# Layer 2's scan: tokens loaded one step ahead, first map of the preparation at tile 2

## The chip, the cores and the metric

The kernel runs on 1 core of one Trainium2 chip. The metric is device microseconds of one execution. In the profile PE is TensorE's matmul track, PEld its weight loads, DVE is VectorE, ACT ScalarE, POOL GpSimd, SP SyncE (here it only issues DMAs). L1548 is line 1548 of the kernel before.

## The reference

Four layers run one after the other on `x` of shape (8, 64, 64, 64), float32: a spectral convolution, a four-way selective scan with a feed-forward part, a second selective scan (the layer that is changed here) and a last layer with scans along both axes. The part of layer 2 that matters:

```python
def spa_ssm(x, in_w, conv_w, conv_b, xproj_w, dt_w, dt_b, Alog, D, out_w):
    xz = xs @ in_w                                   # xs: (8, 4096, 64), 2 x 128 out
    xi, z = (xz[..., :di], xz[..., di:])             # di = 128
    xi = silu(causal_dwconv1d(xi, conv_w, conv_b))   # 4 taps
    dbc = xi @ xproj_w                               # 4 + 16 + 16
    dt = softplus(dbc[..., :dtr] @ dt_w + dt_b)
    B, C = dbc[..., dtr:dtr + 16], dbc[..., dtr + 16:]
    A = -exp(Alog)                                   # (128, 16)
    # h = exp(dt * A) * h + (dt * xi) * B ;  y = sum over the 16 states of h * C
    y = selective_scan(exp(dt[..., None] * A), (dt * xi)[..., None] * B[:, :, None, :], C) + D * xi
    y = y * silu(z)
    return (y @ out_w).reshape(b, h, w, c)
```

## The kernel before

Layer 2's scan (`l2_scan`) cuts the 8 images of 4096 tokens into 32 steps of T = 1024 tokens (image `b`, chunk `c`). The 128 inner channels lie on the partitions. Each step has 16 tiles, one for each state `n`; a tile is 128 x 1024. The loop over all 512 tiles is in `stream`, and it writes the order of the work out by hand (`tc.manual_schedule()`): each engine runs its instructions in the order in which the program issues them.

For tile `i` the work is:

- SP loads a row of B and a row of C, spread over all partitions (`load`, line 1583, 1 MB, into one of 8 buffers `bc`). The load for tile `i + 6` is issued at tile `i`.
- POOL multiplies `du` with B into one of 4 buffers `hb` (line 465), three tiles ahead.
- ACT makes the decay `dA = exp(dt * A)` in one of two PSUM tiles (line 472), two tiles ahead.
- DVE runs the scan (line 481).
- The product with C (line 495) is DVE's in 11 tiles and POOL's in the five of `shared = (1, 4, 7, 10, 13)`.
- From chunk 0 to 2 of an image, ACT copies the last column into the next chunk's `carry` (line 1592).
- PE adds the product to the step's sum `acc` in PSUM, by a matmul with the identity (`gather`, line 287), two tiles later. `acc` is a single buffer: at tile 2 of the next step DVE drains it into `z` (line 1601), and PE starts the new sum with the skip product of `u`. In this one tile the gather is issued behind the scan, in the others ahead of it.

Beside this, a step prepares the next one. `prepare` is a generator, and `stream` starts it at the tile `n == start` and takes one piece of it per tile. A piece that ends in `yield CALM` holds the next piece back until a calm tile, that is, until neither this tile nor the next one is in `shared` (2, 5, 8, 11, 14, 15). The pieces and their tiles are:

| Tile | Piece |
|---|---|
| 1 | Load the tokens `x0` (two DMAs on SP; in chunk 0 also two small memsets on POOL), `yield False` |
| 2 | Nothing (`yield`) |
| 3 | First map: 4 taps and input projection in one, 4 matmuls into the PSUM tile `mm` (line 1548, eight rows of the profile), `yield CALM` |
| 5 | `u` = Silu of it on ACT (line 1551, with a table load), matmul to `dbc` |
| 6 | Copy to `dbl` (1556), B and C to HBM by two DMAs on ACT's queue (1559), matmul to `dt` |
| 8 | `dt` = Softplus (line 396, with a table load) |
| 9 | `du` = `dt * u` on POOL (1569), matmul to `z` (1573) |
| 11 | `z` = Silu (1579, with a table load) |

Once `prepare` is over, the gate of the step before the current one (output matmuls of `z` and of the residual from `x0`, copy by ACT at line 1513, store) runs at tiles 11 to 14. It uses the same single PSUM tile `mm`. The exponential of the decays needs ACT's table again after each of `u`, `dt` and `z`.

Of the kernel before, what the change touches and what calls it, by code (L numbers as in the profile page):

```python
# [10 lines left out]
F32 = mybir.dt.float32  # L11
# [11 lines left out]
T = 1024  # L23
# [226 lines left out]
class Net:  # L250
# [1228 lines left out]
    def l2_scan(self, hx, hy):  # L1479
        nc, tc, d = self.nc, self.tc, self.d  # L1480
        with ExitStack() as ctx:
            pool = lambda n, b, **k: ctx.enter_context(tc.tile_pool(name="l2" + n, bufs=b, **k))
            cp, p1, p2, tp = pool("c", 1), pool("p1", 1), pool("p2", 2), pool("t", 2)
            pp = pool("pp", 1, space=PSUM)
            pools = (pool("bc", 8), pool("hb", 4), pool("hc", 4), pool("h", 3), pool("pe", 2, space=PSUM), pool("pa", 1, space=PSUM))
            hp = pool("h3", 3, space=DRAM)
            w_in, cb, xp, dtw, dtb, A, D, w_out = (
                self.load(cp, "l2_" + n) for n in ("in", "cb", "xp", "dtw", "dtb", "A", "D", "out")
            )
            self.minus_exp(A)  # L1490
            skip = self.diag(cp, "skip", D, 1)

            taps = cp.tile([128, 2, 128], F32, name="taps")
            for m in range(2):
                for r in range(2):
                    j = 3 - 2 * m - r
                    nc.sync.dma_start(taps[r * C : r * C + C, m, :], d["l2_taps"][j : j + 1, :].to_broadcast([C, 128]))
                nc.vector.tensor_tensor(taps[:, m, :], taps[:, m, :], w_in[:, :128], ALU.mult)

            def gate(b, c, y, x0):  # L1500
                q, half = b // 2, slice((b % 2) * C, (b % 2) * C + C)
                yield
                ps = pp.tile([128, T], F32, name="mm")
                self.mm(ps[:C], w_out, y, start=True, stop=False)
                for r in range(2):
                    at, f = slice(r * C, r * C + C), 3 + r + r * 512
                    nc.tensor.matmul(
                        ps[:C, r * 512 : r * 512 + 512], self.ident2[at, :C], x0[at, f : f + 512], start=False, stop=True
                    )
                yield True  # L1510
                yield True
                o = tp.tile([C, T], F32, name="tmp")
                nc.scalar.copy(o, ps[:C])
                nc.scalar.dma_start(hy[q, half, c * T : c * T + T], o)

            carries = {}

            class Step:
                bc_shape, start, early, late = [128, 2, T], 1, 0, False
                shared = (1, 4, 7, 10, 13)  # L1520
                rev = False
                shaped = staticmethod(lambda t: t)
                spread = staticmethod(lambda t, m: t[:, m, :])
                lanes = [(slice(None), A)]

                def __init__(self, b, c):
                    self.b, self.c = b, c

                def ready(self):
                    pass  # L1530

                def prepare(self):
                    b, c = self.b, self.c

                    x0 = self.x0 = p2.tile([128, T + 4], F32, name="x0", bufs=3)
                    for r in range(2):
                        lo = c * T - 3 - r
                        if c == 0:
                            nc.gpsimd.memset(x0[r * C : r * C + C, : 3 + r], 0.0)
                        skip_ = max(0, -lo)  # L1540
                        nc.sync.dma_start(x0[r * C : r * C + C, skip_ : T + 3 + r], hx[b, :, lo + skip_ : c * T + T])
                    yield False
                    yield
                    px = pp.tile([128, T], F32, name="mm")
                    for o in (0, 512):
                        for m in range(2):
                            f = o + 3 - 2 * m
                            nc.tensor.matmul(px[:, o : o + 512], taps[:, m, :], x0[:, f : f + 512], start=m == 0, stop=m == 1)  # L1548
                    yield CALM
                    u = self.u = p2.tile([128, T], F32, name="u")  # L1550
                    nc.scalar.activation(u, px, AF.Silu, bias=cb)
                    pd = pp.tile([128, T], F32, name="mm")[:68]
                    net.mm(pd, xp, u)
                    yield True
                    dbl = p1.tile([68, T], F32, name="dbl")
                    nc.scalar.copy(dbl, pd)
                    self.bc = hp.tile([NS, 2, T], F32, name="bc")
                    for m in range(2):
                        nc.scalar.dma_start(self.bc[:, m, :], dbl[4 + m * NS : 4 + m * NS + NS])
                    pt = pp.tile([128, T], F32, name="mm")  # L1560
                    for r in range(2):
                        at, o = slice(r * C, r * C + 4), slice(r * 512, r * 512 + 512)
                        nc.tensor.matmul(pt[:, o], dtw[at], dbl[at, o], start=True, stop=True)
                    yield CALM
                    dt = self.dt = p2.tile([128, T], F32, name="dt")
                    net.softplus_act(dt, pt, dtb)
                    yield
                    du = self.du = p2.tile([128, T], F32, name="du")
                    nc.gpsimd.tensor_tensor(du, dt, u, ALU.mult)
                    pz = pp.tile([128, T], F32, name="mm")  # L1570
                    for r in range(2):
                        at, f = slice(r * C, r * C + C), 3 + r + r * 512
                        nc.tensor.matmul(
                            pz[:, r * 512 : r * 512 + 512], w_in[at, 128:], x0[at, f : f + 512], start=True, stop=True
                        )
                    yield True
                    yield CALM
                    z = self.z = p2.tile([128, T], F32, name="z", bufs=3)
                    nc.scalar.activation(z, pz, AF.Silu)

                def load(self, n, t):
                    row = self.bc[n : n + 1].rearrange("o m t -> o (m t)")
                    nc.sync.dma_start(t.rearrange("p m t -> p (m t)"), row.to_broadcast([128, 2 * T]))

                def first(self, n):
                    if n == 0:
                        self.carry = p2.tile([128, NS], F32, name="carry") if self.c < 3 else None
                    return carries[self.b][:, n : n + 1] if self.c else 0.0

                def keep(self, n, h):  # L1590
                    if self.carry is not None:
                        nc.scalar.copy(self.carry[:, n : n + 1], h[:, T - 1 : T])
                    if n == NS - 1:
                        carries[self.b] = self.carry

                def skip(self, acc):
                    net.mm(acc, skip[:, 0, :], self.u, start=True, stop=False)
                    return True

                def drain(self, acc):  # L1600
                    nc.vector.tensor_tensor(self.z, acc, self.z, ALU.mult)

                def done(self):
                    net.urgent.append(Task(gate(self.b, self.c, self.z, self.x0)))

            net = self
            with tc.manual_schedule():
                steps = [Step(b, c) for b in range(NB) for c in range(4)]
                self.stream(pools, (6, 3, 6), steps, deque())

    def leaky(self, out, ps):
# [432 lines left out]
```

## Time and profile before

| | |
|---|---|
| Median of 3 runs | 25221.08 us (25216.33 to 25233.35) |
| Profiled execution, its own time | 25231.76 us |
| Its span, first to last instruction | 25229.9 us |
| Busy shares of the span: PE, DVE, ACT, POOL | 85%, 89%, 58%, 87% |
| First and last `DMA_DIRECT2D` of layer 2's token load (line 1541) | 9133.4 and 10797.8 us |
| First and last drain of layer 2's scan (line 1601) | 9220.9 and 10905.2 us |

The profile is of one execution. A busy share is an average over four layers with different limits, so what bears on a change is read from the stretch in which its lines run. A wait "A L1 <- B L2" means that engine A sat idle ahead of its instruction of line L1 until B finished one of line L2. Names stand without their numbers: `x0` appears as `x`.

### The profile page before, as it was taken

The page shows a single profiled execution, that of the slowest core. Times are in us where ns is not written, and L with a number is a line of the kernel's source. Part 1 is how long each engine was busy: PE and PEld are TensorE (multiplying, and loading weights), DVE is VectorE, ACT ScalarE, POOL GpSimd, SP SyncE. Part 2 cuts the span into 40 slices and gives each one's busy share as a digit, 9 for nine tenths or more (in the row PEclk, how much of TensorE's full clock was granted, in tenths as well). Part 3 has the DMA queues.
Part 4 walks back from the last instruction along what each step waited for, and adds up shares of the span by engine and source line. Part 5 has one row for each costly group of instructions (what it writes and reads, how often), then busy time and mean ns, then how long its engine had stood idle before and what let it go on. Part 6 is the DMA issues. An engine that isn't in the chain of part 4 may idle for free. (4 is left out here: it accounts for less than half of the span.)

```text
span 25229.9 us, 193412 instructions
## 1 busy us (share of the span) xinstructions
PE 21360.9 (85%) x53146; PEld 8333.8 (33%) x53146; DVE 22529.7 (89%) x13020; ACT 14745.3 (58%) x18562; POOL 22031.7 (87%) x10775
## 2 busy tenths in 40 slices
PE   8777888888888888888888888888878888888888
PEld 5522333333333323322333333333323333333333
DVE  4379989989989769978999999999989999999999
ACT  4344555555555455524666666666656666666666
POOL 0089999999999759976999999999989999999999
PEclk9888999999999999989999999999989999999999
DMA  2279898889898758842555555555545555555554
GB/s 60 77 279 321 310 317 311 311 313 316 307 315 311 251 194 323 324 134 79 167 170 169 171 166 171 169 170 167 167 155 169 168 170 168 170 168 171 167 171 157
DMA packets 1772400, 5282.72 MB, mean 209 GB/s; under 512 B 536352, under 2 KB 542564, under 8 KB 1703472
## 3 DMA queue, kind: packets, MB, share of 16 engines
q1 hardware_dynamic: 1744176, 5207.00, 61.0%
q10 hardware_dynamic: 27136, 63.34, 0.8%
q8 instruction: 423, 6.93, 0.1%
q14 instruction: 665, 5.45, 0.1%
HBM read 5112.85 MB, written 156.11 MB: 209 GB/s over the span
## 5 line engine op out<-in xcount | busy, mean ns | idle before, releaser
L465 POOL TENSOR_TENSOR hb<-du,bc 128x1024 f32<-128x1024 f32 x4608 | 10749.6, 2357 | 495.7 <-DVE h L481 334.4
L287 PE MATMUL acc<-hc,ident 128*128 128x512 f32 x18816 | 8878.8, 613 | 85.8 <-DVE img L1228 55.9
L472 ACT ACTIVATE dA<-dt,w_A 128x512 f32<-128x512 f32 x8192 | 5662.8, 691 | 4111.9 <-DVE hc L495 3125.9
L481 DVE TENSOR_TENSOR_SCAN dA<-dA,hb 128x1024 f32<-128x1024 f32 x3384 | 7726.0, 2283 | 282.5 <-ACT dA L472 118.4
L287 PE MATMUL acc<-h,ident 128*128 128x512 f32 x7808 | 4553.3, 713 | 2368.4 <-POOL h L495 2368.3
L287 PEld LDWEIGHTS acc<-hc,ident 128*128 128x128 f32 x18816 | 3689.4, 200 | 5292.2 <-issue 4656.8
L465 POOL TENSOR_TENSOR hb<-du,b 128x1024 f32<-128x1024 f32 x2048 | 4869.0, 2402 | 495.0 <-DVE h L481 253.7
L495 DVE TENSOR_TENSOR hc<-dA,bc 128x1024 f32<-128x1024 f32 x3296 | 4034.2, 1224 | 260.8 <-issue 8.9
L472 ACT ACTIVATE dA<-dt,w_l_A 128x1024 f32<-128x1024 f32 x2560 | 2856.5, 1117 | 1187.5 <-DVE hc L495 761.8
L481 DVE TENSOR_TENSOR_SCAN dA<-dA,carry,hb 128x1024 f32<-128x1024 f32 x1320 | 3093.9, 2344 | 172.9 <-ACT carry L1211 111.0
L287 PEld LDWEIGHTS acc<-h,ident 128*128 128x128 f32 x7808 | 1546.1, 215 | 5028.1 <-POOL h L495 3162.1
L481 DVE TENSOR_TENSOR_SCAN h<-dA,hb 128x1024 f32<-128x1024 f32 x1352 | 3081.5, 2279 | 46.0 <-ACT dA L472 40.3
L495 POOL TENSOR_TENSOR h<-h,bc 128x1024 f32<-128x1024 f32 x1312 | 3090.1, 2355 | 14.2 <-DVE h L481 14.2
L495 DVE TENSOR_TENSOR hc<-dA,c 128x1024 f32<-128x1024 f32 x1408 | 1722.5, 1223 | 115.6 <-DMA c<-bc 4.6
L495 POOL TENSOR_TENSOR h<-h,c 128x1024 f32<-128x1024 f32 x640 | 1511.9, 2362 | 8.6 <-ACT carry L1211 8.1
L481 DVE TENSOR_TENSOR_SCAN h<-dA,carry,hb 128x1024 f32<-128x1024 f32 x600 | 1404.4, 2341 | 77.9 <-ACT dA L472 71.6
L472 ACT ACT_TABLE_LOAD x1122 | 1439.5, 1283 | 21.1 <-ACT tmp L997 1.2
L1211 ACT COPY carry<-dA 128x1 f32<-128x1 f32 x1056 | 167.9, 159 | 1735.9 <-DVE hc L495 1674.0
L1911 PE MATMUL mm<-xn,taps 128*128 128x512 f32 x2048 | 937.9, 600 | 34.6 <-POOL xn L1877 32.3
L694 POOL MEMSET xf<- 128x24 f32 x33 | 4.3, 142 | 910.7 <-PE ps L715 731.3
L1926 PE MATMUL mm<-u,w_xp 128*36 128x512 f32 x1024 | 519.1, 632 | 140.5 <-ACT u L1923 135.4
L1946 POOL TENSOR_TENSOR du<-dt,u 128x1024 f32<-128x1024 f32 x256 | 601.4, 2349 | 18.7 <-ACT dt L396 18.7
(310 smaller groups left out, 18613.5 us busy)
## 6 DMA issues: line engine op xcount, KB each, us to landing
bc<-bc SPq DMA_DIRECT2D x4096, 512.0 KB
b<-bc SPq DMA_DIRECT2D x2048, 512.0 KB
c<-bc SPq DMA_DIRECT2D x2048, 512.0 KB
bc<-bc SPq DMA_DIRECT2D x512, 1024.0 KB
tmp<-rs SPq DMA_DIRECT2D x93, 512.0 KB
raw<-x SPq DMA_DIRECT2D x64, 512.0 KB
inv<-rs SPq DMA_DIRECT2D x64, 512.0 KB
tmp<-x SPq DMA_DIRECT2D x192, 128.0 KB
```

What stands on the lines that cost most here:

```text
L287: self.nc.tensor.matmul(o, lhsT, r, start=start, stop=stop)
L465: nc.gpsimd.tensor_tensor(s.shaped(hb[i]), s.shaped(s.du), B.pop(i), ALU.mult)
L472: nc.scalar.activation(dA[i][:, cut], s.dt[:, cut], AF.Exp, scale=A[:, n : n + 1])
L481: nc.vector.tensor_tensor_scan(h[:, way], dA[i][:, way], hb.pop(i)[:, way], s.first(n), ALU.mult, ALU.add)
L495: engine.tensor_tensor(s.shaped(o), s.shaped(h), CC.pop(i), ALU.mult)
L694: nc.gpsimd.memset(x[:, :, HW:], 0.0)
L1211: nc.scalar.copy(self.carry[:, n : n + 1], h[:, last : last + 1])
L1911: nc.tensor.matmul(tokens(px[:, j * W : j * W + W]), taps[k][:, m, j * 128 : j * 128 + 128], xn[:, :, f : f + HW], start=m == 0, stop=m == 1,)
L1926: nc.tensor.matmul(pd, xp[:, k, j, :], u[:, j * W : j * W + W], start=j == 0, stop=j == 1)
L1946: nc.gpsimd.tensor_tensor(du, dt, u, ALU.mult)
```

## The change

It touches `l2_scan` alone.

- Loading the tokens moves out of `prepare` into a method `fetch`. Each step knows the one behind it (`behind`) and calls its `fetch` at the end of its own `prepare`, that is, at tile 11. The tokens of step `s + 1` are thus loaded one step earlier than before, seven tiles ahead of the tile where its preparation starts. Step 0's are loaded ahead of `stream`, and step 1's at the end of step 0's preparation, ahead of the first tile.
- The two empty pieces of `prepare` go, so that its first piece is the first map. `start` becomes 2: the map is issued at tile 2, ahead of the drain and the skip product of that tile, where before it was issued at tile 3 behind that tile's gather. By the rule on calm tiles the later pieces keep their tiles.
- `x0` has four buffers where it had three.

```diff
             class Step:
-                bc_shape, start, early, late = [128, 2, T], 1, 0, False
+                bc_shape, start, early, late = [128, 2, T], 2, 0, False
+                behind = None
...
-                def prepare(self):
+                def fetch(self):
+
                     b, c = self.b, self.c
-
-                    x0 = self.x0 = p2.tile([128, T + 4], F32, name="x0", bufs=3)
+                    x0 = self.x0 = p2.tile([128, T + 4], F32, name="x0", bufs=4)
                     for r in range(2):
                         lo = c * T - 3 - r
                         if c == 0:
                             nc.gpsimd.memset(x0[r * C : r * C + C, : 3 + r], 0.0)
                         skip_ = max(0, -lo)
                         nc.sync.dma_start(x0[r * C : r * C + C, skip_ : T + 3 + r], hx[b, :, lo + skip_ : c * T + T])
-                    yield False
-                    yield
+
+                def prepare(self):
+                    x0 = self.x0
                     px = pp.tile([128, T], F32, name="mm")
...
                     nc.scalar.activation(z, pz, AF.Silu)
+                    if self.behind:
+                        self.behind.fetch()
...
                 steps = [Step(b, c) for b in range(NB) for c in range(4)]
+                for step, other in zip(steps, steps[1:]):
+                    step.behind = other
+                steps[0].fetch()
                 self.stream(pools, (6, 3, 6), steps, deque())
```

## The prediction

> **What bounds the kernel now.** I first looked for the stretch in which the changed lines run. The rows of line 1601 (one drain per step) place layer 2's scan at 9133 to 10907 us of the span: 32 steps of 16 tiles. Nothing outside it is touched, so the whole effect is 31 preparations (steps 1 to 31) times a cost per step. The table by stretches, for 1500 us of it:
>
> ```profile
> core 0: us, PE busy (x) PEld busy (x) DVE busy (x) ACT busy (x) POOL busy (x), PEclk, DMA share, GB/s
> 9300.00:10800.00 1500.00, 1222.24 (x2638) 465.79 (x2639) 1390.15 (x771) 888.70 (x1070) 1402.81 (x620) 0.91 0.86 324
> ```
>
> VectorE (DVE) and GpSimd (POOL) are both busy for 93%; ScalarE (ACT) only for 59%. The question is who makes the two full engines pause. The waits of DVE, ACT, POOL and PE in the scan:
>
> ```profile
> DVE h L481 <- ACT dA L472: 60.3, 29, 3.7
> DVE dA L481 <- ACT carry L1592: 27.4, 21, 2.3
> DVE dA L481 <- ACT dA L472: 10.5, 10, 1.3
> ...
> ACT L1551 <- PE mm L1548: 87.2, 30, 3.3
> ...
> POOL hb L465 <- DVE h L481: 98.7, 79, 2.6
> ...
> PE acc L287 <- DVE z L1601: 136.6, 30, 5.0
> ```
>
> Columns: total us, times, longest. DVE waits about once per step for a decay, ACT waits once per step for the first map (line 1548), and POOL waits for DVE. The timeline of one step shows that this is one chain (start, us, engine, line, and in brackets the idle time before it):
>
> ```profile
> 9657.07 1.21 DVE L1601 TENSOR_TENSOR z<-acc,z 128x1024 f32<-128x1024 f32 x1
> 9658.33 3.78 PE L287 MATMUL acc<-u,skip 128*128 128x512 f32 x4 [4.03 <-DVE z L1601]
> 9665.32 1.11 ACT L472 ACTIVATE dA<-dt,w_l_A 128x1024 f32<-128x1024 f32 x1
> 9666.07 3.60 PE L1548 MATMUL mm<-x,taps 128*128 128x512 f32 x8
> 9669.75 1.28 ACT L1551 ACT_TABLE_LOAD   x1 [3.32 <-PE mm L1548]
> 9671.05 1.11 ACT L1551 ACTIVATE u<-mm,w_l_cb 128x1024 f32<-128x1024 f32 x1
> 9672.23 1.28 ACT L472 ACT_TABLE_LOAD   x1
> 9673.53 1.12 ACT L472 ACTIVATE dA<-dt,w_l_A 128x1024 f32<-128x1024 f32 x1
> 9674.75 2.35 DVE L481 TENSOR_TENSOR_SCAN h<-dA,carry,hb 128x1024 f32<-128x1024 f32 x1 [2.47 <-ACT dA L472]
> ...
> 9677.13 1.12 ACT L472 ACTIVATE dA<-dt,w_l_A 128x1024 f32<-128x1024 f32 x1 [0.25 <-DVE h L481]
> 9678.35 2.36 DVE L481 TENSOR_TENSOR_SCAN dA<-dA,carry,hb 128x1024 f32<-128x1024 f32 x1 [1.26 <-ACT carry L1592]
> ```
>
> The drain (9657.07) belongs to tile 2. PE sat idle 4.03 us for it, then has a backlog: skip product, gathers, and only behind them tile 3's first map, until 9669.7. ACT reaches `u` at tile 5 after the decay of 9665.32 (over at 9666.43) and stands 3.32 us. The decay of tile 7, behind `u` on ACT, is late, so DVE stands 2.47 us before scan 7; tile 8's decay, behind the copy to `dbl`, costs 1.26 us more.
>
> **The change part by part.**
>
> *The map one tile earlier.* Nothing is added on PE: the same eight rows, 3.60 us. At tile 2 the code emits them ahead of the held-back gather with its skip product, so they fall into the idle time that PE spends on the drain, 136.6/30 = 4.55 us on average (4.03 in the step shown). 3.60 fits; were it too long, the rest would come off the backlog behind it, which loses the same 3.60 us at tile 3. Its result is then there about 9658, 8 us before ACT wants it. It needs the tokens (loaded seven tiles before) and the PSUM tile `mm`, free since the copy of the previous gate at tile 14. Were the tokens late, skip product and gathers would queue behind the map on PE. `u` itself stays at tile 5, since the piece behind the map waits for a calm tile, and tiles 3 and 4 are not calm; all later pieces keep their tiles.
>
> ACT in this step then goes: decay 6 over at 9666.43, table load and `u`, carry copy, table load, decay 7. The like chain around `dt` (a table load there and back, one activation, one copy) takes from 9679.38 to 9684.65, 5.27 us, in the same trace, and DVE does not wait behind it. So decay 7 is over at 9671.7; scan 7 could start at 9674.75 - 2.47 = 9672.28. Margin 0.6 us: the 2.47 go. Tile 8: from the end of decay 7 to the end of decay 8 took 9678.25 - 9674.65 = 3.60 us, of which 0.47 were waits. That gives 9674.8 to 9675.3, against scan 8's earliest start 9672.28 + 2.26 = 9674.54: of 1.26 us some 0.3 stay (bounds 0 and 0.8).
>
> Sum: DVE's three rows are 60.3 + 27.4 + 10.5 = 98.2 us, 3.17 per step; less 31 x 0.3 = 9 that stay: 89 us. Bounds for this part: 98.2 - 31 x 0.8 = 73, and 103 if the 4.9 us in which a scan waited for POOL's `hb` go too.
>
> *Does POOL allow it?* From drain to drain the steps at 9603.07, 9657.07, 9712.41 take 54.00 and 55.34 us. Without DVE's two waits (1.92 + 1.25, and 2.47 + 1.26) that is 50.83 and 51.61. POOL's time in the same steps without its waits is 51.0 both times. Three steps in four are of the longer kind (they start from a carry), so DVE needs 51.4 on average plus the 0.3, POOL 51.0: POOL has 0.7 us per step left, and its lead (three `hb` tiles) absorbs the order within a step. Its largest wait (2.61 us, at tile 7) is only the echo of DVE's stall.
>
> *The tokens' load.* Two DMAs per step (`x0`, in the profile `x<-hx`; 0.53 MB, 1.09 to 1.55 us of SP's queue) move from tile 1, between the broadcast loads of tiles 7 and 8, to tile 11 of the step before, behind the load of the next step's tile 1; the two memsets (0.1 us each on POOL, eight steps in all) go with them. Queues passed: SP's, ACT's (nothing issued there), POOL's. Bounds: a gain of at most 1.55 us per step where it stood; a loss of at most 1.55 issue + 0.53 MB / 324 GB/s = 1.6 us transfer, if every byte were on the path. I take 0: SP stood 1317 of 1550 us waiting for free broadcast buffers, and the DMA engines are fuller where the load leaves (share 0.96 to 1.01 in 9600 to 9624, tiles 1 to 8) than where it goes (0.70 to 0.75 in 9624 to 9648, tiles 8 to 15). No new wait arises: with four `x0` tiles the one overwritten was last read by a gate over a step before. Step 1's tokens are loaded while SP waits for the first broadcast rows (9134 to 9150): nothing.
>
> The profiled execution took 25231.76 us (span 25229.9, 1.9 around it), so 25143 for it; the median of the three runs shown is 25221.1, 0.04% below, and 89 off that gives 25132.
>
> **The rivals.**
>
> *POOL becomes the bound* (0.12). If its waits at tiles 4 and 1 stay and only that at tile 7 goes, steps lose 2.61 and 1.86 us, by mean 2.2, times 31 = 69: 25152. For it: POOL at 51.0 is within 1% of DVE. Against: those waits are for DVE's own scans, so DVE is not behind POOL then.
>
> *ACT stays late by its own work* (0.07): the change then does not do what it says. To keep the stall, the chain from 9666.43 to the end of decay 7 would have to take 8.2 us instead of 5.27; the rows of `z` (9689.11 to 9694.05, 4.94) are shorter still. Time with the stall whole: 25221. The Trainium skill (ScalarE: Activation LUTs, "What ACT_TABLE_LOAD costs") says that every switch of table pays a drain of about 1.38 us besides the load's 1.283; by it two switches make the chain 2.8 us longer, 8.0, and the time would be some 12 us less than before, 25209. The trace disagrees: the decay of 9678.27 ends at 9679.38 and the next table load starts at 9679.40, and an activation starts 1.30 us after its load does.
>
> *The loads become the bound, and it is slower* (0.07). A step moves 17.7 MB (324 GB/s x 54.6 us). Shortened to 51.7 it needs 342 GB/s. If the token load, now ahead of the three broadcast loads that follow tile 10's buffer, drove the queue to layer 1's rate (313 GB/s at a share of 0.89), a step would take 56.5 us: +1.9 x 31 = 59, 25280. It decides once POOL waits over 2.9 us per step for `bc`. Against: this stage itself moved 361 and 368 GB/s where its share is near 1, and POOL waited for `bc` 5.3 us in the whole scan.
>
> **How the numbers follow.** Forecast 0.74, POOL 0.12, ACT 0.07, loads 0.07. A change within 0.2% (50 us) is about what a measurement of this kernel cannot tell from none. The first two are faster by more: 0.86; ACT is "same": 0.07; slower 0.07. Range: below, 103 us of gain and half the spread of the runs (17/2): 25110; above, POOL's case and its own uncertainty of a few tens (half of its 69): 25185. The last two cases lie outside, 0.14.
>
> **What would show it.** Right: in the scan ACT's wait for line 1548's map gone (87 us to under 5), PE's wait for the drain under 40 us, DVE's waits for `dA` and `carry` under 15 us, POOL's for DVE well below 98.7, the DMA share near 0.91, drains 51 to 52 us apart. Wrong: waits of DVE for `hb` or of POOL for `bc` of over 1 us per step, a new idle time of the map for `x`, or drains still 54 apart.

## The result and the profile after

| | before | after |
|---|---|---|
| Median | 25222.04 us (25213.87 to 25233.35, 7 runs) | 25150.09 us (25133.53 to 25157.19, 7 runs) |
| Profiled execution | 25231.76 us | 25151.9 us |
| First to last scan of layer 2 | 1742.2 us | 1671.3 us |

The changed kernel is faster: its ratio to the kernel before is 0.9969, 95% interval [0.9958, 0.998], 72 us by the medians. Of the 79.9 us between the two profiled executions, 70.9 lie in layer 2's scan. The other 9 lie outside it, where times differ by as much between any two traces (from the start of layer 2's last scan to the end they go from 14323.5 to 14340.5 us over the ten kernels of this document). In what follows, the length of layer 2's scan, from the start of its first scan instruction to the start of its last, is therefore the finest measure, and the medians are the check on it.

The line numbers move by up to four: the map is now L1550, `u` L1553, the copy to `dbl` L1558, the carry L1596, the drain L1605. The table by stretches of the kernel after (busy time, with the granted clock, DMA share and GB/s at the end):

```profile
core 0: us, PE busy (x) PEld busy (x) DVE busy (x) ACT busy (x) POOL busy (x), PEclk, DMA share, GB/s
9300.00:10700.00 1400.00, 1170.43 (x2576) 440.08 (x2576) 1351.90 (x751) 862.69 (x1039) 1367.23 (x604) 0.94 0.91 339
```

DVE went from 92.7% to 96.6% busy and POOL from 93.5% to 97.7%; the same work is done in less time. The waits of the kernel after in layer 2's scan (total us, times, longest):

```profile
DVE dA L481 <- ACT carry L1596: 29.0, 22, 2.7
DVE dA L481 <- ACT dA L472: 3.8, 4, 1.3
...
ACT tmp L1513 <- PE mm L1507: 65.5, 29, 4.1
...
PE acc L287 <- DVE z L1605: 27.5, 25, 4.9
...
POOL hb L465 <- DVE h L481: 35.9, 50, 1.1
```

ACT's wait for the first map, 87.2 us before, has no row any more. DVE's wait at tile 7 (60.3 us) has none either. What did not go is the pair of rows on top: 27.4 + 10.5 = 37.9 us before, 32.8 now. The timeline of the step that matches the one shown in the prediction says where they sit:

```profile
9629.63 3.60 PE L1550 MATMUL mm<-x,taps 128*128 128x512 f32 x8
...
9632.90 1.21 DVE L1605 TENSOR_TENSOR z<-acc,z 128x1024 f32<-128x1024 f32 x1
...
9634.16 1.98 PE L287 MATMUL acc<-u,skip 128*128 128x512 f32 x4 [0.93 <-DVE z L1605]
...
9641.15 1.11 ACT L472 ACTIVATE dA<-dt,w_l_A 128x1024 f32<-128x1024 f32 x1
...
9642.28 1.28 ACT L1553 ACT_TABLE_LOAD   x1
...
9643.57 1.11 ACT L1553 ACTIVATE u<-mm,w_l_cb 128x1024 f32<-128x1024 f32 x1
...
9646.05 1.12 ACT L472 ACTIVATE dA<-dt,w_l_A 128x1024 f32<-128x1024 f32 x1
...
9647.10 1.00 ACT L1558 COPY dbl<-mm 68x1024 f32<-68x1024 f32 x1
...
9648.02 2.34 DVE L481 TENSOR_TENSOR_SCAN h<-dA,carry,hb 128x1024 f32<-128x1024 f32 x1
...
9649.02 0.16 ACT L1596 COPY carry<-dA 128x1 f32<-128x1 f32 x1 [0.91 <-DVE hc L495]
...
9650.40 1.12 ACT L472 ACTIVATE dA<-dt,w_l_A 128x1024 f32<-128x1024 f32 x1 [1.22 <-DVE h L481]
...
9651.62 2.36 DVE L481 TENSOR_TENSOR_SCAN dA<-dA,carry,hb 128x1024 f32<-128x1024 f32 x1 [1.25 <-ACT carry L1596]
```

The map (9629.63) lies in PE's idle time ahead of the drain. `u` follows its table load, which starts 0.02 us behind the decay. Decay 7 (9646.05) ends 0.85 us before scan 7 starts, and scan 7 has no idle time in front of it.

Tile 8 is another matter. ACT had finished its carry copy at 9649.18, then stood idle 1.22 us *for DVE's scan 7*. Decay 8 (9650.40) starts 0.04 us behind the end of scan 7 (9648.02 + 2.34), and scan 8 has to wait for it, 1.25 us. (The row of scan 8 names the carry copy, which ends at the same time. In `e3_slots` below, scan 8 starts before that copy is over, so it is decay 8 that it waits for.) A decay needs nothing that scan 7 computes. The reading that fits is that decay 8 is written over scan 7's input, that is, into the PSUM tile that decay 7 filled; `e3_slots` tests it. By a count in the compiled program, which no view of the profile shows, 24 of layer 2's 32 steps place decay 8 so. The traces before and after agree step by step: in the 24 steps of chunks 0 to 2, in which ACT reads the scan's last column out of a PSUM tile, decay 8 starts behind the end of scan 7, and in the eight of chunk 3 it starts beside it. The kernel asks for "a tile named `dA`" from a pool with two buffers, and nothing in it enforces that they take strict turns. This was already so in the kernel before; there decay 8 was late anyway (`e5_before_slots`).

### The profile page after: what moved, and what is told of

Its sections match the earlier page's. It is cut to its first block, busy times and chain, and to the rows that moved or that the text cites. A ratio compares the mean times of both kernels' runs of the same rounds, so it can differ in the third digit from the quotient of the medians.

```text
span 25150.1 us, 193387 instructions
## 1 busy us (share of the span) xinstructions
PE 21310.4 (85%) x53146; PEld 8309.4 (33%) x53146; DVE 22523.7 (90%) x13020; ACT 14745.4 (59%) x18562; POOL 21999.8 (87%) x10775
## 5 line engine op out<-in xcount | busy, mean ns | idle before, releaser
L481 DVE TENSOR_TENSOR_SCAN dA<-dA,hb 128x1024 f32<-128x1024 f32 x3384 | 7725.9, 2283 | 281.3 <-ACT dA L472 116.8
L481 DVE TENSOR_TENSOR_SCAN dA<-dA,carry,hb 128x1024 f32<-128x1024 f32 x1320 | 3095.0, 2345 | 163.8 <-ACT carry L1211 114.8
L481 DVE TENSOR_TENSOR_SCAN h<-dA,hb 128x1024 f32<-128x1024 f32 x1352 | 3082.5, 2280 | 29.8 <-ACT dA L472 27.7
L481 DVE TENSOR_TENSOR_SCAN h<-dA,carry,hb 128x1024 f32<-128x1024 f32 x600 | 1404.7, 2341 | 31.8 <-ACT dA L472 28.9
```

The costliest lines, as they stand in the source:

```text
L481: nc.vector.tensor_tensor_scan(h[:, way], dA[i][:, way], hb.pop(i)[:, way], s.first(n), ALU.mult, ALU.add)
```

## The experiments

**The load alone (`e1_load_only`).** The change, with an empty piece put back so that the map stays at tile 3:

```diff
 def prepare(self):
     x0 = self.x0
+    yield
     px = pp.tile([128, T], F32, name="mm")
```

> The changed kernel with an empty piece ahead of the map: tokens still loaded a step ahead, map back at tile 3. Theory (only the time at which the map's result is there matters): no gain, 25222 within 10 us of the kernel before; ACT again waits about 87 us for the map, DVE about 98 us for decays. Rival (the load's move brings something by itself, since it leaves a stretch in which the DMA engines are full): 20 us or more faster than before.

Measured: 25230.64 us against 25232.16 of the kernel before, ratio 1.0 [0.9991, 1.0008]. Layer 2's scan took 1742.2 us, the same as before to the tenth. Its waits are those of before:

```profile
DVE h L481 <- ACT dA L472: 58.1, 28, 3.6
...
ACT L1554 <- PE mm L1551: 84.3, 29, 3.3
```

With the map at tile 3, the load's earlier place has no price and no gain of its own: the theory holds and the rival falls.

**The map alone (`e2_map_only`).** The kernel before, with the load left at tile 1 and one of the two empty pieces removed, so that the map is issued at tile 2 of the step in which its tokens are requested:

```diff
     nc.sync.dma_start(x0[...], hx[...])
 yield False
-yield
 px = pp.tile([128, T], F32, name="mm")
```

> The kernel before with one empty piece taken out: tokens loaded at tile 1 of the same step, map at tile 2, three token buffers. Theory A (the load's place is indifferent, the map's tile is all): as the changed kernel, 25150 within 10 us. Theory B (a load issued at tile 1 lands about 11 us later, since three broadcast loads are ahead of it; the map at tile 2 then blocks PE for some 7 us and skip product and gathers queue behind it, so the copy to dbl and the decay of tile 8 come late): no gain or worse, 25200 to 25270, with about 200 us of PE waiting for x.

Measured: 25280.88 against 25232.16, ratio 1.0019 [1.001, 1.0028], 49 us **slower**; layer 2's scan 1790.2. The waits, and then the timeline of one step (SPq is the issue of the load on SP's queue):

```profile
PE mm L1547 <- DMA x<-hx: 171.3, 25, 10.3
...
DVE dA L481 <- ACT carry L1591: 110.2, 22, 6.3
...
ACT dbl L1555 <- PE mm L287: 129.5, 29, 5.4
```

```profile
9654.80 1.16 SPq L1541 DMA_DIRECT2D x<-hx  x2
...
9666.49 6.18 PE L1547 MATMUL mm<-x,taps 128*128 128x512 f32 x8 [7.67 <-DMA x<-hx]
...
9683.00 1.01 ACT L1555 COPY dbl<-mm 68x1024 f32<-68x1024 f32 x1 [5.37 <-PE mm L287]
...
9686.41 2.36 DVE L481 TENSOR_TENSOR_SCAN dA<-dA,carry,hb 128x1024 f32<-128x1024 f32 x1 [6.32 <-ACT carry L1591]
```

The tokens arrive 11.7 us after their issue (9654.80 to 9666.49). PE works in the order of the program, so the skip product and the gathers queue behind the waiting map. The delay then goes through `dbl` on ACT to DVE, which stands 6.32 us. PE's row for `x` counts up to 10800 us of the span; over the whole scan it is 189.5 us, where Theory B named about 200. Theory A falls and Theory B's mechanism is what the trace shows. Its time was 11 us too low at the upper end (25270), with the kernel before 10 us slower beside this run than in the first runs. The load's earlier place costs nothing, and without it the earlier map is a loss.

**The other direction (`e7_map_tile4`).** The change with two empty pieces, so that the map comes at tile 4:

```diff
 def prepare(self):
     x0 = self.x0
+    yield
+    yield
     px = pp.tile([128, T], F32, name="mm")
```

> The changed kernel with two empty pieces ahead of the map: tokens a step ahead, map at tile 4, so one gather further back in PE's queue than in the kernel before. Theory (DVE's stall is the map's lateness on PE, one for one): one gather is 1.7 us, so ACT's wait grows from 2.9 to 4.6 us per step and DVE's stall with it, 31 x 1.7 = 53 us slower than before, 25275 (25260 to 25290). Rival (the stall has another cause that the change also moved): no difference to the kernel before.

Measured: 25282.18 against 25223.32, ratio 1.0022 [1.0013, 1.0031], 59 us slower; layer 2's scan 1799.2.

```profile
DVE h L481 <- ACT dA L472: 123.4, 31, 6.0
...
ACT L1555 <- PE mm L1552: 143.2, 30, 5.6
```

With the load ahead and the map at tile 2, 3 and 4, the scan took 1671.3, 1742.2 and 1799.2 us. ACT's wait for the map (none, 84.3, 143.2) and DVE's wait at tile 7 (none, 58.1, 123.4) go with it. The theory named 53 us and an ACT wait of 4.6 us per step; the scan grew by 57.0, and ACT's wait is 4.8. The chain map, `u`, decay 7, scan 7 is the mechanism.

**Tile 8: whose fault is it?** Two theories were set against each other. T1: decay 8 waits for its PSUM tile. T2: ACT is late by its own work, the two DMA issues for the rows of B and C between the copy to `dbl` and the decay among it. T1 was tested by giving the two decays names of their own with one buffer each, in layer 2 alone (`e3_slots`):

```diff
-dA[i] = pe.tile([128, T], F32, name="dA")
+if getattr(s, "alternate", False):      # set in layer 2's Step
+    dA[i] = pe.tile([128, T], F32, name=f"dA{i % 2}", bufs=1)
+else:
+    dA[i] = pe.tile([128, T], F32, name="dA")
```

> The changed kernel with layer 2's decays put into two PSUM tiles in strict turn (even and odd tiles), where in 24 of 32 steps the decay of tile 8 stood in the same PSUM tile as that of tile 7 and could start only when scan 7 had read it. Theory T1 (this choice makes the wait that was left at tile 8): DVE's 32.8 us of waits for decay and carry copy fall under 8, 25150 becomes 25118 (plus or minus 8). Rival T2 (ACT is late there by its own work: copy to dbl, two DMA issues, carry copy): nothing, 25150 within 8.

T2 was tested by moving those two issues from ACT's queue to SP's (`e4_sp_rows`):

```diff
-nc.scalar.dma_start(self.bc[:, m, :], dbl[4 + m * NS : 4 + m * NS + NS])
+nc.sync.dma_start(self.bc[:, m, :], dbl[4 + m * NS : 4 + m * NS + NS])
```

> The changed kernel with the two DMAs that write B and C to HBM issued on SP's queue instead of ACT's; that takes 0.88 us from ACT between the copy to dbl and the decay of tile 8. T1 (the decay of tile 8 waits for scan 7 whatever ACT does): DVE's waits stay at about 33 us, the time within 8 us of 25150. T2 (ACT's own work is late): the wait at tile 8 falls from 1.25 to about 0.4 us in some 25 steps, 20 us less, 25130. SP may stand for the copy for up to 3 us per step; its broadcast loads have more slack than that.

Measured: `e4_sp_rows` 25154.89 against 25232.16, ratio 0.9969 [0.9958, 0.9981], the ratio of the change itself; its layer 2 scan is 1671.1 against 1671.3. The waits stay:

```profile
DVE dA L481 <- ACT carry L1596: 31.1, 25, 1.8
...
DVE dA L481 <- ACT dA L472: 1.9, 2, 1.1
```

`e3_slots`: 25133.28 against 25232.16, ratio 0.996 [0.9948, 0.9973]; layer 2's scan 1652.4, 18.9 us shorter than with the change. Its waits, its table by stretches, and its timeline at tiles 7 and 8:

```profile
DVE dA L484 <- ACT dA L475: 7.5, 14, 2.8
DVE dA L484 <- ACT carry L1600: 6.4, 8, 1.8
...
POOL hb L465 <- DVE h L484: 18.5, 30, 1.0
```

```profile
9300.00:10700.00 1400.00, 1178.02 (x2609) 444.13 (x2608) 1369.07 (x760) 875.07 (x1054) 1382.88 (x610) 0.94 0.92 343
```

```profile
9634.71 2.34 DVE L484 TENSOR_TENSOR_SCAN h<-dA,carry,hb 128x1024 f32<-128x1024 f32 x1
...
9635.89 1.12 ACT L475 ACTIVATE dA<-dt,w_l_A 128x1024 f32<-128x1024 f32 x1
...
9637.10 2.36 DVE L484 TENSOR_TENSOR_SCAN dA<-dA,carry,hb 128x1024 f32<-128x1024 f32 x1
```

Decay 8 (9635.89) now runs *beside* scan 7, which ends at 9637.05, and scan 8 follows with no idle time. T1 holds as the cause of the 1.25 us, and T2 falls. The size is smaller than T1 expected: 13.9 us of waits stay where under 8 were expected, so 18.9 of 32.8 went, and the median lies 7 us above T1's range. By tile, the waits at tile 8 fell from 31.5 us (24 waits) to 6.7 (11, of which 2.8 us in step 0), but those at tile 0 rose from 1.3 to 7.2. POOL is 98.8% busy in this kernel.

**Is the strict turn worth something without the change (`e5_before_slots`)?** The kernel before with the edit of `e3_slots`:

> The kernel before with layer 2's decays in two PSUM tiles in strict turn, nothing else. Theory (with the map late the decay of tile 8 is late by ACT's own work as well; the trace of before shows it held by scan 7 for only 0.25 us): 0.25 us in 23 steps, about 6 us, so within 10 us of the kernel before. Rival (the two causes add): 20 us or more faster, as the same edit brought on top of the change.

Measured: 25231.26 against 25223.32, ratio 1.0002 [0.9993, 1.0011]; layer 2's scan 1741.9 (before 1742.2).

```profile
DVE h L484 <- ACT dA L475: 52.7, 24, 3.7
DVE dA L484 <- ACT dA L475: 33.2, 31, 2.4
...
DVE h L484 <- POOL hb L465: 16.8, 7, 2.4
```

Nothing, so the rival falls. As long as the map is late, decay 8 is late by it, whichever tile it goes to. The same edit is worth 18.9 us of layer 2's scan behind the change and 0.3 in front of it.

**The strict turn in all scans (`e6_slots_all`, `e8_slots_sp`).** Layer 1 runs the same `stream`, and by the count in the compiled program 160 of its 2048 decays go into the tile of the decay in front (layer 3: none of 4096). In the trace of the change, 127 decays of layer 1 stand until the scan in front of them ends, and none of layer 3; with the strict turn none of layer 1 does. `e6_slots_all` is the change with the strict turn everywhere. `e8_slots_sp` adds the edit of `e4_sp_rows`.

```diff
-dA[i] = pe.tile([128, T], F32, name="dA")
+dA[i] = pe.tile([128, T], F32, name=f"dA{i % 2}", bufs=1)
```

> The changed kernel with the decays of all three scans in two PSUM tiles in strict turn. In layer 1, 160 of 2048 decays stood in the same PSUM tile as the one before them, in layer 3 none. Theory: what held in layer 2 (some 20 us for 24 such decays, 0.9 us each) holds in layer 1: 160 x 0.9 = 140 us more than the edit in layer 2 alone, so about 24990, with DVE's waits for ACT's carry copies and decays in layer 1 (236 us in the changed kernel) down by over 100. Rival: in layer 1 the shared tiles differ and GpSimd or the loads take over: under 50 us more, 25085 or above.

> The changed kernel with the decays of all three scans in strict turn and, in layer 2, the two DMAs of B and C on SP's queue. With the PSUM tiles in turn, ACT's own chain is what should be left of the wait at tile 8 (13.9 us in the whole scan with layer 2's decays in turn). Theory: taking 0.88 us from that chain leaves under 6 us of DVE waits for ACT in layer 2's scan, which is some 8 us off 25098, at the edge of what can be measured. Rival (what is left is not ACT's chain): 10 us or more of these waits stay.

Measured: `e6_slots_all` 25097.54 against 25223.32, ratio 0.9949 [0.9937, 0.9962]. Layer 1's scan, 7333.6 us with the change, took 7289.1, so 44 us went where 140 were expected, and the rival's time (25085 or above) is the one that came. The 44 us are themselves rough: the eight kernels that leave layer 1 alone have it at 7321.5 to 7338.8. DVE's waits in layer 1, first of the change, then of `e6_slots_all`:

```profile
DVE dA L481 <- ACT carry L1211: 172.8, 132, 3.6
...
DVE dA L481 <- POOL hb L465: 78.1, 21, 65.2
...
DVE dA L481 <- ACT dA L472: 61.7, 50, 2.3
```

```profile
DVE dA L484 <- ACT dA L475: 119.4, 88, 3.9
DVE dA L484 <- POOL hb L468: 106.2, 59, 65.3
...
DVE dA L484 <- ACT carry L1214: 8.3, 12, 1.9
```

ACT's two rows shrink from 234.5 to 127.7 us, by over 100 as the theory said, and 28 of that come back as waits for POOL. So of the rival's reasons GpSimd is in part borne out. The rest of the difference between these rows and the 44 us was not followed up.

`e8_slots_sp`: 25087.98 against 25232.62, ratio 0.9941 [0.9928, 0.9955], the fastest kernel that was run, though its interval overlaps that of `e6_slots_all`, and the extra edit shows no effect (layer 2's scan 1648.1 against 1650.0). The waits of layer 2's scan:

```profile
DVE dA L484 <- ACT carry L1599: 8.1, 11, 1.3
DVE dA L484 <- ACT dA L475: 5.0, 4, 3.2
...
ACT tmp L1516 <- PE mm L1510: 95.8, 30, 4.5
```

Expected were under 6 us for DVE; 13.1 are left, so the rival holds. In `e6_slots_all` 5.7 us of these waits sat at tile 8 and 6.1 at tile 0. Here a single one of 3.2 us, in step 0, is left at tile 8, and 9.9 us sit at tile 0. So the two issues seem to have cost ACT something at tile 8, but what went there came back at tile 0. Tile 0 comes behind the gate's copy at tile 14, for which ACT waits 51.1 us before, 65.5 with the change, 83.7 in `e3_slots` and 95.8 here. That the gate is the next late piece is a guess from these numbers and was not tried; `e7_map_tile4`, where ACT waits 75.0 us for it, is slow for another reason.

## Why the prediction was right, and the term that was off

- **What bounds the scan**: right. The late map held both full engines; moving it by a tile in either direction moves the scan by 57 to 71 us.
- **The map fits PE's idle time, its result is early**: right. The wait for the drain fell from 136.6 to 27.5 us (under 40 was named), ACT's wait for the map from 87.2 to nothing, and `u` still comes at tile 5.
- **Decay 7 in time, margin 0.6 us, tile 7's 60.3 us go**: right; margin 0.85 us in the step shown, no row left.
- **Tile 8, "of 1.26 us some 0.3 stay (bounds 0 and 0.8)"**: this is the step that failed. The whole 1.25 us stayed in the 24 steps of chunks 0 to 2: 32.8 us in 26 waits, 24 of them here, where the sum had 9 and the signs of being right named under 15. The working took decay 8's start from ACT's own chain. The timeline of before held the hint: `[0.25 <-DVE h L481]` in front of decay 8, an ACT instruction waiting for a *scan*. It was counted among the waits to be taken off, as if it would go with the stall. In the kernel after it is 1.22 us: ACT's work ahead of decay 8 came earlier by more than scan 7 did. The bound of 0.8 was too low for the same reason: with decay 8 behind the end of scan 7, one whole activation (1.12 us) and the hand-overs are exposed.
- **The sum**: 98.2 - 32.8 = 65.4 us of DVE's waits went, where 89 were forecast. With the 4.9 us for POOL's `hb`, which the upper bound held and whose row is gone, it is 70.3; the scan measures 70.9. The forecast of 25132 against 25150 is off by this term. The scan's 70.9 us also lie just under the 73 that the prediction gave as the lower bound of this part. That the time still falls inside the stated range is in part luck: the range's upper end, 25185, was taken from POOL's case, which did not come.
- **DVE's floor of 50.8 to 51.6 us a step**: right. With most waits of tile 8 gone, the drains of `e3_slots` are mostly 51.2 to 51.7 us apart (50.9 to 53.5 over the whole scan, but for 45.5 at its very end), as here:

```profile
9516.23 1.21 DVE L1609 TENSOR_TENSOR z<-acc,z 128x1024 f32<-128x1024 f32 x1
...
9567.88 1.21 DVE L1609 TENSOR_TENSOR z<-acc,z 128x1024 f32<-128x1024 f32 x1
...
9619.58 1.21 DVE L1609 TENSOR_TENSOR z<-acc,z 128x1024 f32<-128x1024 f32 x1
...
9671.16 1.21 DVE L1609 TENSOR_TENSOR z<-acc,z 128x1024 f32<-128x1024 f32 x1
```

  In the kernel after they are mostly 51.2 in the steps without a carry to copy and 52.0 or 52.8 in the others, where the prediction's sign was 51 to 52. Tile 8's 1.25 us is the largest part of that.
- **The load's move at 0**: right as a time (`e1_load_only`). What it makes possible was told only as "were the tokens late"; `e2_map_only` puts a number on it, 49 us of loss.
- **The rivals**: POOL did not bind the change. Its waits for DVE fell to 35.9 us, 1.2 us per step where the prediction left it 0.7, and it is 97.7% busy; in `e3_slots` these waits are 18.5 us and it is 98.8%. ACT's own work did not keep the stall. The trace after shows the table load 0.02 us behind the decay and `u` 1.29 us behind the load's start. The drain of about 1.38 us at each switch that the Trainium skill gives (ScalarE: Activation LUTs, "What ACT_TABLE_LOAD costs") has no place there, and the 12 us of gain that it would have left are not what was measured. (The prediction's own figures for it, 8.2 less 8.0 us in 31 steps, give 6 rather than 12.) The loads did not become the bound: the DMA share rose from 0.86 to 0.91 and POOL has no wait for `bc`.

## What to carry to other kernels

When two engines are both over 90% busy and still pause, look for a half-idle engine at the start of their waits (here POOL waited for DVE, and DVE for ACT), and move the piece that makes it late into an idle hole of the engine that makes the piece. Then check that the inputs of the moved piece arrive that much earlier, for without them the same move was a loss here. A wait that looks impossible by the data (a decay for a scan that it does not feed) was a buffer being reused here: repairing the chain in front of it did not shorten it (0.25 us before, 1.22 after), so price such a wait apart. And edits to one chain need not add: an edit worth nothing ahead of another was worth 19 us behind it.

## What was not expected of the hardware

The skip product on PE got faster though nothing in it changed: its matmul rows went from a median of 1061 ns to 592 ns, first before, then after (durations are min/median/max in ns):

```profile
L287 PE MATMUL acc<-u,skip x104: 593/1061/1223, 9331.7 to 10699.2; 128*128 128x512 f32 x104
```

```profile
L287 PE MATMUL acc<-u,skip x108: 592/592/697, 9321.3 to 10680.6; 128*128 128x512 f32 x108
```

Before, these rows came behind 4.0 to 5.0 us of idle time; after, the map fills it, mostly under 2 us are left, and the granted clock of the stretch rises from 0.91 to 0.94. During the skip product at 9658.33 before, behind 4.03 us of idle time, the granted clock is 0.50; during the one at 9634.16 after, behind 0.93 us, it is 1.00. The Trainium skill (TensorE: Matmul & The Clock Gate, "Part 1: The HAM clock gate") says that the clock falls to half behind an idle window of about 3.4 us and rises after as much work. The fall agrees with these numbers. A four-row skip product takes 1.98 us instead of up to 3.78. In `e2_map_only` the same is seen on the map itself, 6.18 us behind an idle time of 7.67 instead of 3.60. So an idle hole on PE cost twice here: the hole of 4 to 5 us, and up to 1.8 us for the slower rows behind it.

The second is the landing time of the token load: 11.7 us from issue to use for 0.53 MB, in a queue that already holds the broadcast loads of the tiles ahead, though its issue takes 1.16 us. That those loads are what delays it was not tested by a run.
